# A gated graph layer on one core: completion counts of their own for two streams of transfers, and five groups of rows instead of two on the SyncE queue

## The chip, the cores and the metric

The kernel runs on one core of a Trainium2 chip. The core has five engines, each with an instruction queue of its own: PE (matrix products), DVE (vector work), ACT (activations and copies), POOL (which here only issues gathers) and SyncE, whose queue (SPq) issues nearly all plain transfers. Engines and transfers wait for one another by semaphores. The metric is device time in microseconds (us); lower is better.

## The reference

The layer works on a graph of 12,500 nodes with 128 features and 400,000 edges, which arrive sorted by their target node. Cut to what matters:

```python
h = jnp.maximum(_layernorm(x), 0.0)
s, d = src, dst                                            # 400,000 edges
m = relu(concat([h[s], h[d], edge_attr]) @ w1 + b1) @ w2 + b2
agg = segment_sum(m, d, num_segments=12500)
gi = agg @ w_ih + b_ih
gh = h @ w_hh + b_hh
r = sigmoid(gi_r + gh_r);  z = sigmoid(gi_z + gh_z)
n = tanh(gi_n + r * gh_n)
out = x + (1 - z) * n + z * h
```

## The kernel before

**Tiles.** A tile is 128 edges. 8 tiles make a group `k` (1024 edges); there are `NP` = 391 groups. The main loop runs over half-groups `u` from 0 to 781, here called half-steps, so group `k` belongs to half-steps 2k and 2k + 1. A first stage normalises the nodes, keeps them transposed on the chip (`hT_all`) and writes the products `h @ w1[0:128]` to a table `A` and `h @ w1[128:256] + b1` to a table `B`, both in device memory.

**What a group needs.** Since the edges are sorted by target, the targets of a group lie in a window of 32 nodes (two of them, 8 apart, for the two halves of the tiles).
- The window's rows of `B` are brought into a buffer `RW` by two transfers of 16 KB (`window_rows`, L602), four groups ahead; there are four such buffers.
- A buffer `L` (three of them, each for two groups) receives two transfers of 256 KB from `fetch`: the places of the targets (L563, from `dstP`: two rows, each repeated over 32 partitions) and the transposed edge features (L566, from `eaP`). `fetch(k // 2 + 3)` stands at half-step u = 2k of every second group, that is once in four half-steps, and waits until PE has used the buffer.
- DVE turns the places in `L` into a one-hot matrix (`onehot_T`, L575), three groups ahead of the group's last step. PE multiplies `L` by `RW` (L673), which gives the target's and the edge features' part of the message.
- The source's part, rows of `A`, comes in one of four ways, below. DVE adds it and applies the relu in one custom instruction (L701). PE then sums the messages per node by a one-hot product (L724), and every 14 groups a block of nodes is finished by a generator (`node`) that is advanced step by step.

**Four ways for the source's rows.** By default POOL gathers them: one indirect DMA for each tile (L156), 8 for a group, into one of 11 buffers `G`. A gather waits until the add of the group 11 earlier on POOL's list has freed its buffer. The table `SPREAD` takes some groups away from POOL and spreads them evenly over the loop: 27 to DVE and 28 to ACT, which copy the columns of `hT_all` one by one (L967, L960; PE multiplies them afterwards), and some to SyncE, which issues a transfer of 512 B for each of the 1024 rows (L952) into one buffer, `G_sp`. Before each 32 rows SyncE loads 32 row addresses into registers (L945).

**What sets the order.** The order is written out by hand: what each engine does follows the program. `run_jobs` spreads the work of a one-by-one group evenly over the half-steps between its start and its end, four phases to a half-step, four rows at a time for SyncE. A SyncE group `k` has to be through at half-step 2k - 8, and the next one starts at 2k + 2. The first starts at u = 24. `START` and `SPREAD` give the groups their places:

```python
lo, hi = START[m] // 2 + 2, NP - {"dve": 7, "act": 5, "sp": 12}[m]
for i in range(n):
    k = lo + int((i + 1) * (hi - lo) / n)
```

**Semaphores of transfers.** Unless told otherwise, every transfer that SyncE issues counts up one of eight semaphores, taken in turn. Before a transfer is issued, the one that used the same semaphore eight transfers earlier must have landed. All of SyncE's transfers are in one such ring: rows, windows, places, features, the nodes' loads and stores.

Of the kernel before, what the change touches and what calls it, by code (L numbers as in the profile page):

```python
# [11 lines left out]
I32 = mybir.dt.int32  # L12
# [5 lines left out]
ALU = mybir.AluOpType  # L18
# [11 lines left out]
V = 32  # L30
# [9 lines left out]
QP = 2  # L40
# [12 lines left out]
PIECE = 128  # L53
STEP = {"act": 4, "dve": 8, "sp": 4}
ROW = 4 * D
SPREAD = {"dve": 27, "act": 28, "sp": 2}
START = {"dve": 14, "act": 4, "sp": 24}
NR = 12672

# [4 lines left out]
def tile_gnn(ctx: ExitStack, tc: tile.TileContext, x, src, srcT, dstT, dstP, eaT, eaP, w1, b1, w2T, b2,  # L64
             wih, bih, whh, bhh, out):
    nc = tc.nc
# [23 lines left out]

    mode, order = {}, {m: [] for m in SPREAD}
    for m, n in SPREAD.items():
# [3 lines that stand above are left out]
# [171 lines left out]
    node_of = const.tile([2 * V, NP], F32, name="node_of")  # L267
# [75 lines left out]
    with tc.tile_pool(name="pp", bufs=3) as pp:  # L343
# [77 lines left out]
        def chunk(q):  # L421
            b, c = chunks[q]
            i0, n = bats[b]
            return b, i0, c, min(n, c + 4), PB(b), (i0 + c) * 128
# [4 lines left out]
        for q in range(NC + 3):  # L429
            if q < NC:  # L430
                b, i0, c, e, P, n0 = chunk(q)
# [3 lines left out]
            if 1 <= q <= NC:  # L435
                b, i0, c, e, P, n0 = chunk(q - 1)
# [6 lines left out]
            if q >= 3:  # L443
                b, i0, c, e, P, n0 = chunk(q - 3)
# [3 lines left out]
            if q < NC:  # L448
                b, i0, c, e, P, n0 = chunk(q)
# [4 lines left out]
            if 1 <= q <= NC:  # L454
                b, i0, c, e, P, n0 = chunk(q - 1)
# [12 lines left out]
            if q >= 3:  # L468
                b, i0, c, e, P, n0 = chunk(q - 3)
                if e == bats[b][1]:  # L470
                    nc.sync.dma_start(nodes(A, i0, e, P), asb[b][:P, :e, :])
            if 2 <= q <= NC + 1:
                b, i0, c, e, P, n0 = chunk(q - 2)
# [13 lines left out]
    dlast = p3.tile([128, BLOCKS[-1][1] + 128], F16, name="dlast", bufs=1)  # L487
# [63 lines left out]


    Ls, OH, RT, HE, SEG = ({} for _ in range(5))
    hand = {}

    def fetch(q):
        if q * QP >= NP:
            return
        n = min(QP, NP - q * QP)
        c = slice(q * QP * 512, (q * QP + n) * 512)  # L560
        Ls[q] = p3.tile([128, QP * 512], F32, name="L")
        p = dstP[:, c]
        nc.sync.dma_start(  # L563
            Ls[q].bitcast(I32)[:2 * V, :n * 512],
            bass.AP(tensor=p.tensor, offset=p.offset, ap=[list(p.ap[0]), [0, V], [1, n * 512]]))
        nc.sync.dma_start(Ls[q][2 * V:, :n * 512], eaP[:, c])  # L566

    def onehot_T(k):
        if k >= NP:
            return  # L570
        c = slice((k % QP) * 512, (k % QP + 1) * 512)
        o, i = Ls[k // QP][:2 * V, c], Ls[k // QP].bitcast(I32)[:2 * V, c]
        n = k - BLOCKS[-1][0]
        if n < 0:
            nc.vector.tensor_scalar(o, i, node_of[:, k:k + 1], None, op0=ALU.is_equal)  # L575
        else:
            nc.vector.tensor_scalar(o, i, node_of[:, k:k + 1], 0.0, op0=ALU.is_equal, op1=ALU.add,
                                    accum_out=dlast[:2 * V, n:n + 1])


    bases = {}
# [433 lines left out]
    for q in range(3):  # L1015
        fetch(q)
# [4 lines left out]
    def stages(u):  # L1021
        if u + 7 >= 0:
            raw_stats(u + 7)
        if u + 6 >= 0:
            raw_fin(u + 6)
            raw_h(u + 6)
        if u % 2 == 0:
            onehot_T(u // 2 + 3)
        elif u > -7:
            onehot(u // 2 + 3)  # L1030
        if u + 4 >= 0:
            raw_turn(u + 4)
        if u + 3 >= 0:
            pre(u + 3)
        if u + 2 >= 0:
            add(u + 2)
            relu(u + 2)
# [18 lines left out]
    for u in range(NU):  # L1056
        k, h = divmod(u, 2)
        gathers(u)
        if h == 0:
            window_rows(k + 4)  # L1060
            if k % QP == 0:
                fetch(k // QP + 3)
            if k and k == BLOCKS[block(k)][0]:
                nodes_left.append([node(block(k) - 1), 2 if k < BLOCKS[-1][0] else 1])
            if k % PLACE == 1:
                indices(k // PLACE + 2)
            if k % PLACE == 5:
                place(k // PLACE + 1)
                dst_tile(k // PLACE + 2)
            if k == 6:  # L1070
                late_setup()
            if k == 20:
                store_stats()
            if k == NP - 20:
                check_windows()
        if u == min(START.values()) - 2:
            nc.vector.tensor_scalar(at[:NJ, :], at[:NJ, :], place_of[:, 0:1], place_of[:, 1:2],
                                    op0=ALU.mult, op1=ALU.add)
# [123 lines left out]
    f = nc.values_load(flag[0:1, 0:1], min_val=0, max_val=1)  # L1202
# [67 lines left out]
```

## Time and profile before

| | |
|---|---|
| median of 3 runs | 3404.46 us (3404.36 to 3407.26) |
| the profiled execution | 3403.76 us |
| its span, first to last instruction | 3401.8 us |
| ACT busy | 3079.4 us |
| POOL busy | 2566.1 us |
| PE busy | 2417.4 us |
| DVE busy | 2225.1 us |
| gathers (POOL) | 2669 |
| single rows (SyncE) | 2048 |
| bytes moved | 335.44 MB |

The profile's first part lists busy time by engine. Instructions that only issue a transfer, load registers or wait are not counted as busy, so SyncE has no row there at all; its waits are an answer of their own, in which "SPq L952 <- DMA L<-in_dstP" reads: SyncE, at line 952, waited until the transfer into L from dstP had landed. Idle time of another engine ends either by a releaser, which is named, or by "issue", where the engine waited for nothing that the profile shows. A row of a group reads: line, engine, operation, output and inputs, count, then busy us, mean ns of one, idle us before them and what ended it.

### The profile page before, as it was taken

What the parts mean: (1) busy time and instruction counts of PE and PEld (TensorE: products, weight loads), DVE (VectorE), ACT (ScalarE), POOL (GpSimd) and SP (SyncE); (2) the same over time, 40 slices, a digit from 0 to 9 for tenths busy, and PEclk for the clock granted to TensorE, in tenths of its full rate; (3) what the DMA queues carried; (4) which work ended last, traced back from release to release, by engine and by line L of the source; (5) the groups of instructions that cost most, each with busy time, mean ns of one, the idle gap of its engine ahead of it and who ended that gap; (6) DMA issues with size and microseconds to landing.
All of it is one profiled execution on the core that took longest, in us unless ns stands there. A gap on an engine that the chain in (4) does not pass through costs nothing. (4 is left out here: it accounts for less than half of the span.)

```text
span 3401.8 us, 88642 instructions
## 1 busy us (share of the span) xinstructions
PE 2417.4 (71%) x13113; PEld 1563.7 (46%) x13113; DVE 2225.1 (65%) x16468; ACT 3079.4 (91%) x29057; POOL 2566.1 (75%) x2678
## 2 busy tenths in 40 slices
PE   7567777777677767776777667676677767766767
PEld 7444444444445444544444444444444434444445
DVE  8556666666676666666666666666666666666665
ACT  7699999999999998999899988988988898898984
POOL 7777777777777777777777777777777777777776
PEclk9777887887887778777877877788777778777878
DMA  6434444434443333343434433443433334343332
GB/s 213 106 88 93 97 100 99 101 94 100 102 98 94 98 99 95 95 101 97 98 93 99 98 94 93 96 96 93 98 93 92 95 94 99 92 97 96 92 92 73
DMA packets 191316, 335.44 MB, mean 99 GB/s; under 512 B 66753, under 2 KB 112384, under 8 KB 190729
## 3 DMA queue, kind: packets, MB, share of 16 engines
q0 software_dynamic: 85408, 175.09, 23.0%
q1 hardware_dynamic: 105177, 154.58, 16.4%
q14 instruction: 478, 3.92, 0.4%
q8 instruction: 109, 1.79, 0.2%
q10 hardware_dynamic: 144, 0.07, 0.0%
HBM read 309.24 MB, written 20.24 MB: 97 GB/s over the span
## 5 line engine op out<-in xcount | busy, mean ns | idle before, releaser
L156 POOL DMA_INDIRECT G<-A,src_i x2600 | 2498.9, 961 | 796.2 <-issue 753.7
L960 ACT COPY HE_act<-hT_all 128x4 uint8 x28672 | 2886.8, 189 | 51.4 <-issue 27.0
L967 DVE SCALAR_TENSOR_TENSOR both<-hT_all 128x4 uint16 x13824 | 1173.4, 153 | 988.5 <-issue 980.7
L673 PE MATMUL pre<-RW,L 128*128 128x256 f32 x3128 | 1132.4, 488 | 229.8 <-DVE RB L701 220.6
L673 PEld LDWEIGHTS pre<-RW,L 128*128 128x128 f32 x3128 | 660.6, 236 | 506.1 <-DVE RB L701 234.0
L724 PE MATMUL seg<-RB,OH 128*32 128x129 f32 x6250 | 603.9, 324 | 380.0 <-DVE RB L701 349.7
L724 PEld LDWEIGHTS seg<-RB,OH 128*32 128x32 f32 x6250 | 333.1, 125 | 820.4 <-DVE RB L701 532.7
L701 DVE CUSTOM_DVE_ANT_0 RB<-pre,G 128x1024 f32<-128x1024 f32 (+1 forms) x326 | 394.5, 1210 | 62.7 <-DMA G<-A,src_i 49.2
L575 DVE TENSOR_SCALAR L<-L,node_of 64x512 f32<-64x512 int32 x382 | 186.7, 489 | 9.7 <-DMA L<-in_dstP 9.4
L719 PE MATMUL seg<-zrow 1*128 1x129 bf16 x196 | 45.3, 231 | 164.4 <-DVE OH L623 164.2
L623 DVE TENSOR_TENSOR OH<-dloc,seg 128x256 f32<-128x256 f16 (+1 forms) x392 | 159.5, 407 | 0.5 <-issue 0.5
L750 PE MATMUL nd<-spot,sums 128*128 128x40 f32 x782 | 116.6, 321 | 1.2 <-DVE sums L733 1.2
L750 PEld LDWEIGHTS nd<-spot,sums 128*128 128x128 f32 x782 | 112.4, 231 | 10.5 <-issue 9.0
L710 ACT ACTIVATE RB<-pre 128x1024 f32<-128x1024 f32 x64 | 65.0, 1015 | 52.4 <-PE pre L684 52.4
L809 ACT ACTIVATE gt<-nd 128x512 f32<-128x512 f32 (+2 forms) x28 | 16.4, 585 | 96.5 <-PE nd L803 96.5
L972 DVE COPY HE_dve<-both 128x512 uint8<-128x512 uint8 x216 | 96.6, 447 | 7.4
L684 PEld LDWEIGHTS pre<-w1a,HE_act 128*128 128x128 f32 x448 | 88.4, 245 | 11.6
L684 PEld LDWEIGHTS pre<-w1a,HE_dve 128*128 128x128 f32 x432 | 87.9, 252 | 12.1
L684 PE MATMUL pre<-w1a,HE_act 128*128 128x128 f32 x448 | 86.4, 327 | 0.0
L684 PE MATMUL pre<-w1a,HE_dve 128*128 128x128 f32 x432 | 85.1, 333 | 0.0
L156 POOL DMA_INDIRECT G<-in_x,src_i x69 | 65.9, 954 | 21.8 <-issue 20.7
L233 PE MATMUL nd<-w1b,hT_all 128*128 128x128 f32 x224 | 45.5, 346 | 43.3 <-DVE xb L835 43.3
(177 smaller groups left out, 1383.9 us busy)
## 6 DMA issues: line engine op xcount, KB each, us to landing
L<-in_dstP SPq DMA_DIRECT2D x195, 256.0 KB
L<-in_eaP SPq DMA_DIRECT2D x195, 256.0 KB
G<-A,src_i POOLq DMA_INDIRECT x2600
G_sp<-A SPq DMA_DIRECT2D x2048, 0.5 KB
RW<-B SPq DMA_DIRECT2D x782, 16.0 KB
xb<-in_x SPq DMA_DIRECT2D x26, 256.0 KB
out<-xb SPq DMA_DIRECT2D x26, 256.0 KB
xs<-in_x SPq DMA_DIRECT2D x11, 512.0 KB
```

The costliest lines, as they stand in the source:

```text
L156: nc.gpsimd.indirect_dma_start(out=G[k][:, j, a, :], out_offset=None, in_=table, in_offset=bass.IndirectOffsetOnAxis(ap=src_i[c][:, i:i + ...
L575: nc.vector.tensor_scalar(o, i, node_of[:, k:k + 1], None, op0=ALU.is_equal)
L623: nc.vector.tensor_tensor(o, d.to_broadcast(shape), i.to_broadcast(shape), op=ALU.is_equal)
L673: nc.tensor.matmul(p[:, 2 * i:2 * i + 2, :], Ls[k // QP][:, c0:c0 + 128], RW[k % 4], start=True, stop=not raw)
L684: nc.tensor.matmul(p[:, 2 * i + a, :], cols, w1a, start=False, stop=n + 1 == len(l) or l[n + 1][1] != j)
L701: nc.vector._custom_dve(TENSOR_ADD_SAT, out=o, in0=p, in1=G[k].rearrange("p j a f -> p (j a) f")[:, c, :], s0=float("inf"), s1=0.0)
L710: nc.scalar.activation(o, p, AF.Relu)
L724: nc.tensor.matmul(p[r0:r0 + V, :D + 1], OH[k][:, j, a, :], RB[k % 2][:, 2 * j + a, :D + 1], start=False, stop=all(b != a for _, _, b in r ...
L750: nc.tensor.matmul(p[:, bass.ds(offs[i], V + SHIFT)], sums[:, slot(b, i), :D], spot[:, i % 2, :], start=False, stop=i == len(offs) - 1)
L960: nc.scalar.copy(he[:, e * 4:e * 4 + 4], column(v))
L967: nc.vector.scalar_tensor_tensor(both[:, (e0 % PIECE + i) // 2, :], column(vals[i + 1]), 256.0, column(vals[i]), op0=ALU.mult, op1=ALU.add)
L972: nc.vector.tensor_copy(he[:, p0 * 4:(p0 + PIECE) * 4].rearrange("p (n c b) -> p n c b", c=2, b=4), both.bitcast(U8).rearrange("p n (b c) ...
```

## The change

The change has two parts. The places and features of `L` no longer count up the ring of eight: each of the three buffers gets a semaphore of its own, which both transfers of a fetch raise by 16, and DVE waits for it explicitly before the first one-hot of the buffer. And SyncE gets five groups in place of two; by the code above these are 87, 160, 233, 306 and 379 where they were 196 and 379. The groups of DVE and ACT stay where they are.

```diff
-SPREAD = {"dve": 27, "act": 28, "sp": 2}
+SPREAD = {"dve": 27, "act": 28, "sp": 5}
...
+    landed = [tc.alloc_semaphore(f"landed{i}") for i in range(3)]
...
     def fetch(q):
...
-        nc.sync.dma_start(
-            Ls[q].bitcast(I32)[:2 * V, :n * 512],
-            bass.AP(tensor=p.tensor, offset=p.offset, ap=[list(p.ap[0]), [0, V], [1, n * 512]]))
-        nc.sync.dma_start(Ls[q][2 * V:, :n * 512], eaP[:, c])
+        for fetched in (
+                nc.sync.dma_start(
+                    Ls[q].bitcast(I32)[:2 * V, :n * 512],
+                    bass.AP(tensor=p.tensor, offset=p.offset, ap=[list(p.ap[0]), [0, V], [1, n * 512]])),
+                nc.sync.dma_start(Ls[q][2 * V:, :n * 512], eaP[:, c])):
+            fetched.then_inc(landed[q % 3], 16)
+            tc.no_tile_sem_insts.add(fetched.ins.name)
+            tc.add_to_no_dep_group(f"places{q}", fetched.ins)
 
     def onehot_T(k):
         if k >= NP:
             return
+        q = k // QP
+        if k % QP == 0:
+            nc.vector.wait_ge(landed[q % 3], 32 * (q // 3 + 1))
...
+        tc.declare_no_dep(made.ins, group=f"places{q}", reason="behind the wait for the landing")
+        if k % QP == 0:
+            tc.declare_fence(made.ins, group=f"places{q}")
```

More of the change, by code (lines that the diff above doesn't have):

```diff
@@ L574, in onehot_T @@
         if n < 0:
-            nc.vector.tensor_scalar(o, i, node_of[:, k:k + 1], None, op0=ALU.is_equal)
+            made = nc.vector.tensor_scalar(o, i, node_of[:, k:k + 1], None, op0=ALU.is_equal)
         else:
-            nc.vector.tensor_scalar(o, i, node_of[:, k:k + 1], 0.0, op0=ALU.is_equal, op1=ALU.add,
-                                    accum_out=dlast[:2 * V, n:n + 1])
+            made = nc.vector.tensor_scalar(o, i, node_of[:, k:k + 1], 0.0, op0=ALU.is_equal, op1=ALU.add,
+                                           accum_out=dlast[:2 * V, n:n + 1])
+        tc.declare_no_dep(made.ins, group=f"places{q}", reason="behind the wait for the landing")
+        if k % QP == 0:
+            tc.declare_fence(made.ins, group=f"places{q}")
     bases = {}
```

## The prediction

> **What bounds the kernel now.** I read the page first, then the stretches of the span engine by engine, then who waited for whom, and last SyncE's own waits, which the page does not list among its engines.
>
> ```profile
> span 3401.8 us, 88642 instructions
> PE 2417.4 (71%) x13113; PEld 1563.7 (46%) x13113; DVE 2225.1 (65%) x16468; ACT 3079.4 (91%) x29057; POOL 2566.1 (75%) x2678
> L156 POOL DMA_INDIRECT G<-A,src_i x2600 | 2498.9, 961 | 796.2 <-issue 753.7
> ```
>
> ACT has the largest share, but POOL is the engine that never rests: its idle time is put down to "issue", the gap that its own sequencer leaves between two gathers. One gather costs (2498.9 + 796.2) / 2600 = 1.267 us. The stretches (PE, PEld, DVE, ACT, POOL, each with its count) confirm it:
>
> ```profile
> 400.00:800.00 400.00, 295.01 (x1616) 188.22 (x1615) 275.20 (x2095) 386.22 (x3777) 303.04 (x315) 0.82 0.41 98
> 1200.00:1600.00 400.00, 288.11 (x1559) 186.00 (x1558) 267.95 (x2050) 374.74 (x3651) 303.66 (x317) 0.80 0.39 97
> 2800.00:3200.00 400.00, 278.71 (x1493) 174.94 (x1493) 257.78 (x1948) 359.74 (x3465) 303.41 (x318) 0.77 0.39 95
> ```
>
> POOL issues 315 to 318 gathers in every 400 us, while ACT falls from 386 to 360: ACT has room, POOL has none. The sum of waits agrees from the other side, since the add on DVE does run into gathered rows that have not landed:
>
> ```profile
> DVE RB L701 <- DMA G<-A,src_i: 49.2, 31, 3.7
> ```
>
> So POOL's row of gathers sets the time, and every other engine follows at a distance. Next comes SyncE's queue (SPq). These are its waits while it brings rows one by one, and the rows (tile G_sp) with their first and last start:
>
> ```profile
> SPq L952 <- DMA L<-in_dstP: 865.4, 150, 8.1
> SPq L563 <- PE pre L673: 180.4, 55, 14.1
> SPq L952 <- DMA L<-in_eaP: 89.1, 170, 1.5
> SPq L602 <- DMA L<-in_dstP: 71.5, 13, 6.9
> SPq L602 <- DMA B<-xb: 56.3, 24, 3.1
> SPq L563 <- PE pre L684: 54.7, 9, 13.2
> SPq L119 <- DMA L<-in_dstP: 46.4, 8, 6.7
> SPq L108 <- DMA L<-in_dstP: 36.4, 6, 6.8
> SPq L602 <- PE pre L673: 20.9, 13, 4.2
> ```
>
> ```profile
> L952 SPq MOVE G_sp<-A x2048: 29/29/38, 229.9 to 3276.3; - x187
> L952 SPq DMA_DIRECT2D G_sp<-A x2048: 224/228/643, 229.9 to 3276.4; - x187
> ```
>
> The stretch is 3276.3 - 229.9 = 3046.4 us long. In it SyncE waits 865.4 + 71.5 + 46.4 + 36.4 = 1019.7 us for the places (L from dstP) to land, 89.1 us for the features (L from eaP), and 180.4 + 54.7 + 20.9 = 256.0 us for PE. Only the last is slack: there SyncE is early. The other 3046.4 - 1019.7 - 89.1 - 256.0 = 1681.6 us are its instructions and small waits (B's store of 56.3 us among them). SyncE, no engine of the page's first part, is thus taken for 2790 of 3046 us and is the second limit, close behind POOL.
>
> **The change, part by part.** *Gathers.* Three groups of 8 tiles leave POOL: 24 gathers x 1.267 = 30.4 us less. As long as nothing else is slower, that is the gain. The add on DVE reads G_sp in place of G and costs the same.
>
> *Rows.* By the code, SyncE's groups are now 196 and 379, and become 87, 160, 233, 306 and 379. The first still starts at half-step u = 24 and the last still has to be through by u = 2 x 379 - 8 = 750, so 5120 rows stand where 2048 stood, in the same 726 half-steps of the program. The price of a row and of its registers:
>
> ```profile
> 1536.45 1.21 SPq L952 DMA_DIRECT2D G_sp<-A  x4
> ```
>
> ```profile
> L945 SPq TENSOR_LOAD <-at x64: 1876/2142/2377, 227.6 to 3229.5; - x64
> L945 DVEq EVENT_SEMAPHORE  x1: 21/21/21, 188.1 to 188.1; - x1
> ```
>
> Four rows back to back take 1.21 us from the first start to the last end, and the last lasts 0.228, so one row every (1.21 - 0.228) / 3 = 0.327 us. 3072 more rows are 1005 us, and 96 more loads of 32 registers at 2.142 us are 206 us. SyncE's work becomes 1681.6 + 1005 + 206 = 2893 us, against 3046.4 - 30.4 = 3016 us that POOL's new pace would leave it. It fits, with 123 us over, only if the waits for places and features go. Everything hangs on that.
>
> *Semaphores.* Places and features leave the ring of eight semaphores. A transfer of the ring waits until the one eight before it has landed; so far, six transfers could follow a pair of L before the seventh waited for the places. Here is that, in one fetch:
>
> ```profile
> 1505.43 0.58 SPq L563 DMA_DIRECT2D L<-in_dstP  x1
> 1506.07 0.51 SPq L566 DMA_DIRECT2D L<-in_eaP  x1
> 1506.68 10.14 SPq L952 DMA_DIRECT2D G_sp<-A  x8
> 1517.93 0.35 SPq L740 DMA_DIRECT2D xb<-in_x  x1
> ```
>
> Eight rows take 10.14 us where 8 x 0.327 = 2.6 would do. After the change eight transfers can follow, and the ninth waits for the first of these eight. So the question is when that first row lands, and the packets answer it (first line: 1509.6 to 1513.6 us; second: its hardware queue; third: 1514.5 to 1514.7 us):
>
> ```profile
> DMA packets 150, 0.38 MB, mean 95 GB/s; under 512 B 60, under 2 KB 60, under 8 KB 149
> ```
>
> ```profile
> q1 hardware_dynamic: 34, 0.14, 10.7%
> ```
>
> ```profile
> DMA packets 15, 0.01 MB, mean 56 GB/s; under 512 B 7, under 2 KB 13, under 8 KB 15
> ```
>
> Six rows are issued by 1506.68 + 6 x 0.36 = 1509. In the four microseconds from 1509.6 no packet of 512 B moves at all (the counts under 512 B and under 2 KB are both 60); the queue moves 34 packets in 0.14 MB, the 4 KB pieces of L. Then, within 0.2 us, 13 - 7 = 6 packets of 512 B move: the six rows, together, behind L. They land when the places land. The wait therefore does not go; it changes its name, from the places to the first row behind them.
>
> [...]
>
> What it becomes: there are 726 / 4 = 182 fetches in the stretch, so 1019.7 / 182 = 5.6 us each today. Two more transfers pass before the stop, 2 x 0.327 = 0.65 us: 4.95 us if the first row lands with the places, and 0.52 us more (89.1 / 170, how much later the features land) if it lands behind the features. I take the middle, 5.2 us, or 946 us. The features' own 89.1 us go.
>
> *The explicit wait on DVE.* 196 instructions of about 0.021 us, 4 us on an engine that is not the limit: nothing. The same wait stood on L575 before; behind it in DVE's queue stand the one-hot, the adds and DVE's share of hand-made columns, which PE and ACT await. If DVE were the limit it would cost those 4 us; less than nothing it cannot cost, since the instruction it frees still waits for the same landing. Three more index rows in the preamble go out before the stretch, beside the transposes and loads of the first stage; exposed, they would cost 3 x 0.327 = 1 us.
>
> *Sum.* 2893 + 946 = 3839 us for the stretch: SyncE becomes the bound, its 256 us of slack are used up, and PE and DVE wait for windows (RW) and places that it issues late. Two corrections. L shares its DMA engines with POOL's gathers, and POOL slows to about 3046 / 3839 = 0.8 of its rate. In the quiet window the 34 packets occupied 0.107 x 16 x 4.0 = 6.85 us, or 0.20 us each; if L's tail stands on two engines, one for each of the two rows of places, they took 4.0 x 2 / 34 = 0.235 us for each; over 36 packets that is 1.2 us per fetch if POOL were gone altogether, and some more since a packet itself is stretched. With a fifth of POOL gone I take 0.45 us per fetch, 82 us in all (ends: 0 and 310, the latter for 1.7 us each). And SyncE starts the stretch ahead of its users: L is asked for 6 half-steps before its one-hot, 6 x 3046 / 726 = 25 us, and takes some 10 to land, so 15 us pass before anyone waits. So 3839 - 82 - 15 = 3742 us, 696 us more than now: a span of 3401.8 + 696 = 4098 us. The profiled execution took 3403.76 us with its span of 3401.8, and the median of the runs is 3404.46, so the same within 1 us; I say 4095.
>
> **Rivals.** *The wait really goes* (faster). If rows behind L landed in their usual time, SyncE would need 2893 us plus little, POOL would stay the bound, and the time would be 3404 - 30 = 3374 us. For it speaks that 1109 us of waiting carry L's name. Against it stand the packets above. It decides where the stall per fetch falls under (3016 - 2893) / 182 = 0.7 us, from 5.6 today; at 0.85 us the gain is just gone.
>
> *L lands far sooner.* With POOL waiting for buffers in turns, L could have its DMA engines to itself: at 1.7 to 3 us less per fetch the stretch is 310 to 550 us shorter, and the time 3630 to 3870 us. For it: gathers and L do run beside each other. Against it: the POOL work per group stays, and it is only spread over a fifth more time.
> [...]
>
> *More than the sum.* If the first row always lands behind the features and POOL's slowing brings nothing, the stretch is 2893 + 182 x 5.5 = 3894 us, and the time 4240.
>
> **How the numbers follow.** Main case, SyncE the bound and 3870 to 4260 us: 0.84. L much sooner, 3630 to 3870: 0.06. The wait goes, 3374: 0.08. Both cancel at about 3404: 0.02. Runs of this kernel agree to about 0.1%, so 0.2% is about what can be told from no change. Faster 0.08, same 0.02, slower 0.90. The range of 8 in 10 is the main case with its bounds: 3840 to 4270.
>
> **What would show it.** Right: SyncE's waits name G_sp or RW where they named L, some 5 us per fetch; its waits for PE all but vanish; POOL waits for RB's add; the last row starts near 3970 instead of 3276.3; PE and DVE wait for RW or L. [...]

## The result, and the profile after

The changed kernel takes 4172.09 us (median of 4 runs, 4165.45 to 4174.29), the one before 3405.17 us on the same chip: a ratio of 1.225, 95% interval 1.2235 to 1.2264. It is slower by 767 us. The main case of the prediction, SyncE's queue as the bound, came about; its 4095 us were 77 us too low.

The page of the changed kernel, by engine, and the groups whose idle time tells most (busy, mean ns of one, idle before and its releaser):

```profile
span 4172.5 us, 94686 instructions
PE 2550.5 (61%) x13113; PEld 1623.6 (39%) x13113; DVE 2235.3 (54%) x16468; ACT 3086.7 (74%) x29057; POOL 2535.9 (61%) x2654
L156 POOL DMA_INDIRECT G<-A,src_i x2576 | 2468.6, 958 | 1506.7 <-DVE RB L712 747.0
L684 PE MATMUL pre<-RW,L 128*128 128x256 f32 x3128 | 1244.3, 529 | 1443.2 <-DMA RW<-B 1277.7
L583 DVE TENSOR_SCALAR L<-L,node_of 64x512 f32<-64x512 int32 x382 | 188.3, 493 | 726.6 <-DMA L<-in_eaP 726.1
```

The busy time of ACT, DVE and POOL is what it was, to within 1.2%; only the span grew. POOL, which waited 2.6 us for the add before, now waits 747.0 us for it to free a buffer. PE waits 1277.7 us for windows and DVE 726.1 us for L: all of them wait for what SyncE issues late. PE's granted clock is lower too (0.746 in the mean, 0.796 before) and its busy time 5.5% longer; but PE is busy for 61% of the span, and SyncE hardly waits for it any more, as its waits further down show. POOL's pace in two stretches (the POOL column is the fifth after the length) falls from 317 gathers in 400 us to about 250:

```profile
1200.00:1600.00 400.00, 230.67 (x1178) 141.01 (x1178) 203.32 (x1542) 277.04 (x2692) 238.61 (x250) 0.74 0.31 75
2800.00:3200.00 400.00, 227.16 (x1156) 142.54 (x1155) 203.68 (x1548) 296.84 (x2856) 234.84 (x245) 0.72 0.31 75
```

SyncE's own waits while it brings rows, from 230 to 4071 us, and the rows' first and last start:

```profile
SPq L963 <- DMA G_sp<-A: 881.0, 170, 8.1
SPq L613 <- DMA B<-xb: 57.9, 26, 3.6
SPq L565 <- PE pre L684: 22.3, 13, 8.0
SPq L565 <- PE pre L695: 13.0, 2, 12.5
SPq L247 <- DMA RW<-B: 7.7, 1, 7.7
SPq L963 <- DMA RW<-B: 7.3, 3, 4.2
SPq L613 <- PE pre L684: 6.0, 5, 4.8
```

```profile
L963 SPq MOVE G_sp<-A x5120: 29/29/39, 230.2 to 4071.0; - x197
```

None of SyncE's waits carries L's name any more. Instead SyncE waits 881.0 us, 170 times, for rows of its own. The stretch is 4071.0 - 230.2 = 3840.8 us where it was 3046.4, and the waits for PE, which were 256.0 us, have shrunk to 22.3 + 13.0 + 6.0 = 41.3 us.

### The profile page after: what moved, and what is told of

Its sections match the earlier page's. It is cut to its first block, busy times and chain, and to the rows that moved or that the text cites. A ratio compares the mean times of both kernels' runs of the same rounds, so it can differ in the third digit from the quotient of the medians.

```text
span 4172.5 us, 94686 instructions
## 1 busy us (share of the span) xinstructions
PE 2550.5 (61%) x13113; PEld 1623.6 (39%) x13113; DVE 2235.3 (54%) x16468; ACT 3086.7 (74%) x29057; POOL 2535.9 (61%) x2654
## 2 busy tenths in 40 slices
DMA packets 196745, 335.84 MB, mean 80 GB/s; under 512 B 69444, under 2 KB 118147, under 8 KB 196111
## 3 DMA queue, kind: packets, MB, share of 16 engines
q0 software_dynamic: 84640, 173.51, 18.4%
## 5 line engine op out<-in xcount | busy, mean ns | idle before, releaser
L156 POOL DMA_INDIRECT G<-A,src_i x2576 | 2468.6, 958 | 1506.7 <-DVE RB L712 747.0
L684 PE MATMUL pre<-RW,L 128*128 128x256 f32 x3128 | 1244.3, 529 | 1443.2 <-DMA RW<-B 1277.7
L684 PEld LDWEIGHTS pre<-RW,L 128*128 128x128 f32 x3128 | 726.1, 259 | 1755.6 <-issue 1350.1
L735 PE MATMUL seg<-RB,OH 128*32 128x129 f32 x6250 | 619.7, 331 | 75.3 <-DVE RB L712 55.6
L583 DVE TENSOR_SCALAR L<-L,node_of 64x512 f32<-64x512 int32 x382 | 188.3, 493 | 726.6 <-DMA L<-in_eaP 726.1
L712 DVE CUSTOM_DVE_ANT_0 RB<-pre,G 128x1024 f32<-128x1024 f32 x323 | 392.6, 1216 | 28.9 <-PE pre L684 24.9
L810 PE MATMUL nd<-DEG,brow 34*128 34x512 f32 (+2 forms) x112 | 77.7, 780 | 4.9 <-ACT gt L820 4.5
L814 PE MATMUL nd<-TOT,w2ih 128*128 128x512 f32 (+2 forms) x112 | 72.1, 732 | 0.0
## 6 DMA issues: line engine op xcount, KB each, us to landing
L<-in_dstP SPq DMA_DIRECT2D x195, 256.0 KB
L<-in_eaP SPq DMA_DIRECT2D x195, 256.0 KB
xb<-in_x SPq DMA_DIRECT2D x26, 256.0 KB
out<-xb SPq DMA_DIRECT2D x26, 256.0 KB
```

The source lines that it names most:

```text
L156: nc.gpsimd.indirect_dma_start(out=G[k][:, j, a, :], out_offset=None, in_=table, in_offset=bass.IndirectOffsetOnAxis(ap=src_i[c][:, i:i + ...
L583: made = nc.vector.tensor_scalar(o, i, node_of[:, k:k + 1], None, op0=ALU.is_equal)
L684: nc.tensor.matmul(p[:, 2 * i:2 * i + 2, :], Ls[k // QP][:, c0:c0 + 128], RW[k % 4], start=True, stop=not raw)
L712: nc.vector._custom_dve(TENSOR_ADD_SAT, out=o, in0=p, in1=G[k].rearrange("p j a f -> p (j a) f")[:, c, :], s0=float("inf"), s1=0.0)
L735: nc.tensor.matmul(p[r0:r0 + V, :D + 1], OH[k][:, j, a, :], RB[k % 2][:, 2 * j + a, :D + 1], start=False, stop=all(b != a for _, _, b in r ...
L810: nc.tensor.matmul(pg, brow[:, c], DEG[:, :w], start=True, stop=False)
```

## Experiments

**The semaphores alone.** Two groups as before:

```diff
-SPREAD = {"dve": 27, "act": 28, "sp": 5}
+SPREAD = {"dve": 27, "act": 28, "sp": 2}
```

In the expectations from here on, a ring that rows share with L is not the ring of eight semaphores. It stands for the hardware queue q1 of the profile: in the fetch of the prediction q1's 34 packets from 1509.6 to 1513.6 us are L's, and the rows' six of 512 B are among its 13 from 1514.5 to 1514.7 us.

> Two groups of rows as before, semaphores of L as after. Theory (a row issued behind L shares a ring with it and lands when L lands): the time stays at 3405 us within 0.3%, since POOL is the bound in both, and SyncE's waits only change their name: about 1110 us in the name of L become 850 to 1000 us in the name of G_sp and RW. Rival (the semaphores free SyncE): the time is the same too, but SyncE waits less than 250 us for any transfer, and its waits for PE rise from 256 us to over 1000.

Measured: 3402.76 us against 3400.49, ratio 1.0003 (0.9993 to 1.0013): no difference. SyncE's waits in its stretch:

```profile
SPq L963 <- DMA G_sp<-A: 525.1, 99, 8.5
SPq L613 <- DMA G_sp<-A: 379.9, 63, 8.9
SPq L565 <- PE pre L684: 282.3, 70, 14.2
SPq L613 <- DMA B<-xb: 60.5, 28, 3.6
SPq L751 <- DMA G_sp<-A: 54.9, 12, 6.6
SPq L613 <- PE pre L684: 52.0, 22, 5.8
SPq L565 <- PE pre L695: 49.2, 7, 13.5
```

525.1 + 379.9 + 54.9 = 959.9 us of waiting for rows stand where 1109 us of waiting for L stood; the waits for PE rise from 256 to 383.5 us. The semaphores by themselves free about 130 to 150 us of SyncE's queue, not a thousand. The wait changes its name, and the rival in which it goes has fallen.

**The five groups alone.** The kernel before with the same one line changed from 2 to 5, L on the ring of eight.

> Five groups of rows, semaphores as before. Theory: SyncE is the bound, and the stall at each L is whole, 5.6 us for the places and 0.5 for the features, where the changed kernel has about 5.2: 2893 + 1020 + 89 = 4002 us of stretch against the changed kernel's 3841, so about 4330 us. Rival (the semaphores do nothing at all): 4172 us. Rival (it is the new semaphores and the explicit wait on DVE that cost the time, not the rows): near 3405 us.

Measured: 4360.59 us against 3400.49, ratio 1.281 (1.2767 to 1.2853).

```profile
SPq L952 <- DMA L<-in_dstP: 984.1, 172, 8.8
SPq L952 <- DMA L<-in_eaP: 92.1, 170, 1.5
SPq L602 <- DMA B<-xb: 56.8, 26, 3.1
```

```profile
L952 SPq MOVE G_sp<-A x5120: 29/29/39, 231.3 to 4260.5; - x197
```

The stretch is 4029.2 us (4002 expected), the time 31 us above the 4330 expected, and both rivals are far off. The slowdown comes from the rows; the semaphores win back 4029.2 - 3840.8 = 188 us of it.

**The places in two transfers.** If the rows stand behind L on one queue, L's time on it must be made shorter. In the same fetch, from 1506.6 to 1508.9 us, the queue moved

```profile
q1 hardware_dynamic: 70, 0.27, 39.8%
```

or 0.398 x 16 = 6.4 packets at a time; the 34 from 1509.6 to 1513.6 us, at 10.7%, are 1.7 at a time. By the trace's packets, over all fetches of the kernel before, 12.4 of the queue's 4 KB packets run at once 3 us after the places' transfer starts, and 2.0 after 6 us. The places are two rows, each repeated, into 64 partitions. That the two rows make this thin end, and that a transfer for each row would run more of its pieces at once, was my estimate; no run had shown it. The same bytes, then, in one more transfer, with DVE's wait raised to match:

```diff
-                nc.sync.dma_start(
-                    Ls[q].bitcast(I32)[:2 * V, :n * 512],
-                    bass.AP(tensor=p.tensor, offset=p.offset, ap=[list(p.ap[0]), [0, V], [1, n * 512]])),
+                *(nc.sync.dma_start(
+                    Ls[q].bitcast(I32)[V * a:V * (a + 1), :n * 512],
+                    dstP[a:a + 1, c].to_broadcast([V, n * 512])) for a in range(2)),
...
-            nc.vector.wait_ge(landed[q % 3], 32 * (q // 3 + 1))
+            nc.vector.wait_ge(landed[q % 3], 48 * (q // 3 + 1))
```

> The changed kernel, with the places as two transfers of 32 partitions, one for each row, in place of one of 64 partitions. [...] The stall goes, the stretch is 2893 us + 182 x 0.6 for the third transfer = 3002 us, which just fits POOL's 3016, and the time is 3370 to 3420 us. Rival (rows wait for something other than their ring, the general load of the DMA engines): the same bytes move, so about 4172 us plus 182 x 0.6 = 4280.

Measured: 3373.97 us against 3400.49, ratio 0.9917 (0.9897 to 0.9937). It beats both kernels, the one before by 0.8%. SyncE's waits in its stretch, its rows, and POOL's pace in one stretch:

```profile
SPq L613 <- DMA B<-xb: 57.2, 26, 3.3
SPq L565 <- PE pre L684: 47.9, 15, 11.4
SPq L963 <- DMA G_sp<-A: 44.5, 83, 1.2
SPq L565 <- PE pre L695: 13.8, 3, 7.9
SPq L613 <- PE pre L684: 11.8, 6, 5.5
```

```profile
L963 SPq MOVE G_sp<-A x5120: 29/29/38, 214.8 to 3252.3; - x197
```

```profile
1200.00:1600.00 400.00, 283.87 (x1528) 181.22 (x1528) 266.20 (x2022) 372.26 (x3603) 303.51 (x317) 0.80 0.38 98
```

Waiting for rows falls from 881.0 to 44.5 us with the same five groups, and POOL is back at 317 gathers in 400 us. By the trace's landings, the first row behind L lands 4.8 us after the places' transfer starts (median over the fetches that a row follows), where it took 10.2 us in the changed kernel. What held the rows was the shape of the places' transfer, not the general load: the bytes are the same (335.84 MB in the changed kernel, 335.88 here). The semaphores differ too: until a transfer of the places has landed, its semaphore rises in 3 steps at most in the kernel before, and in up to 16 where the same kernel has the split. For a single row it rises in 2 at most. How many DMA engines a transfer had, the profile does not record.

**The split alone.** The same split in the kernel before, with two groups and the shared semaphores.

> The kernel before with the same split of the places, its two groups and the shared semaphores kept. Theory: the time stays at 3405 us within 0.3% (POOL is the bound), and SyncE's waits in the name of L fall from 1109 us to under 250, its waits for PE rise by about as much. Rival (SyncE's stalls already cost the kernel before something): 20 us or more are gained.

Measured: 3399.68 us against 3400.49, ratio 0.9996 (0.9987 to 1.0006). Over the whole span:

```profile
SPq L563 <- PE pre L672: 900.4, 158, 13.2
SPq L601 <- PE pre L672: 362.1, 67, 18.0
SPq L951 <- DMA L<-in_eaP: 98.9, 116, 2.5
```

About a thousand microseconds of SyncE's queue change from stalls behind L into waits for PE, and the time does not move: SyncE was not the bound of the kernel before. POOL was: the add on DVE still waits for gathered rows, for 42.2 us here and 49.2 us in the kernel before, and the split kernel, with 24 gathers fewer, is 26.5 us faster.

```profile
DVE RB L700 <- DMA G<-A,src_i: 42.2, 29, 4.3
```

**Fewer gathers beside L.** One correction of the prediction was that L lands sooner when POOL slows. Here POOL gathers half of the tiles from group 40 on; the messages of the other half lack their source's part.

```diff
+        if k >= 40:
+            nc.gpsimd.memset(G[k][:, :, 1, :], 0.0)
         for u in (2 * k, 2 * k + 1):
             for t, j, a in unit_tiles(u):
+                if k >= 40 and a:
+                    continue
```

> The changed kernel, but from group 40 on POOL gathers only every other tile of its groups (those of the first half of the window) and clears the rest with one memset, so the messages of the cleared tiles lack their source's part; it is there to see how much POOL's gathers hold up L. Half of the gather traffic is gone beside L. Theory of the prediction (L shares its DMA engines with the gathers and lands sooner when they thin out, up to 1.7 us per fetch if all were gone): 0.6 to 0.9 us less stall per fetch, 881 us of waiting for rows becomes 730 to 780, and the time 4020 to 4070 us. [...]

Measured in one execution: 4090.01 us. SyncE's waits for rows, and what the two queues moved:

```profile
SPq L967 <- DMA G_sp<-A: 818.5, 170, 7.9
```

```profile
q1 hardware_dynamic: 111327, 156.18, 14.1%
q0 software_dynamic: 46880, 96.10, 10.5%
```

The gathers fall from 173.51 to 96.10 MB, and the wait from 881.0 to 818.5 us, 0.37 us a stop; the time falls by 82 us. Beside L itself, too, they are halved: 4 to 12 us after L is issued, 13.9 packets of the gathers' queue start per microsecond, where 26.0 did in the changed kernel. The expectation missed: the effect is there, at about half the size I gave it. The first row behind L lands after 9.8 us (mean) in place of 10.2, so L's pace is mostly its own.

**Three and four groups.** The changed kernel with "sp": 3, and with 4.

> The changed kernel with three groups of rows in place of five. Theory: each group costs SyncE 1024 x 0.327 + 32 x 2.142 = 403 us, so its work is 2893 - 2 x 403 = 2086 us, plus 182 x 5.2 = 946 us of stalls: 3032 us, just what POOL's pace (3046 - 10 = 3036) leaves. The time is at the knee, 3390 to 3440 us. Rival (the cost is not in proportion to the rows but comes with the new placing of the groups from 87 on): near the five groups' 4172 us, or near 3395 us with SyncE waiting for PE more than before.

> The changed kernel with four groups of rows. Theory: 403 us of SyncE's work per group on top of a full queue, so one group less than five takes 403 us off the stretch of 3841: 3438 us, and the time is 4172 - 403 = 3769 us, within 30 us. Rival (the stalls grow with the rows behind L): more than 30 us off this line.

Measured: 3463.16 us with three (ratio 1.0155, 1.0115 to 1.0195) and 3814.61 us with four, in one execution. SyncE's rows, three groups first, then four:

```profile
L963 SPq MOVE G_sp<-A x3072: 29/29/39, 232.5 to 3348.9; - x192
```

```profile
L963 SPq MOVE G_sp<-A x4096: 29/29/39, 230.4 to 3702.7; - x196
```

The stretches are 3116.4, 3472.3 and 3840.8 us for three, four and five groups, so a group costs 356 and 368 us, not the 403 of its instructions, and both points lie above the line (by 23 us over the range's end, and by 46 us). Both expectations missed, and the rivals for three groups lie further off still. The price of the rows held: without the waits for rows and for PE the stretches differ by 388 and 404 us. The stalls did not stay as they were, but against the rival they grow with fewer rows. With three groups waiting behind L is

```profile
SPq L613 <- DMA G_sp<-A: 719.1, 124, 8.8
SPq L963 <- DMA G_sp<-A: 122.4, 25, 7.7
SPq L751 <- DMA G_sp<-A: 101.6, 23, 6.2
```

943.1 us, against 922.0 with four and 881.0 with five. The stall is a landing that has to be waited out, and what SyncE does meanwhile comes off it: by the traces' landings, a stop is 3.6 us long with five groups where SyncE loads registers between L and the stop, and 5.5 us where it does not. But that does not explain the difference, for with three groups such loads fall before 48 of 179 stops and with five before 49 of 181. Most of it lies in the stops without a load, 5.9 us with three groups and 5.5 with five. Why these shorten stays open.

**The split with the shared semaphores.** Five groups and two transfers for the places, but L back on the ring of eight semaphores; against the split kernel it tells what semaphores of its own are worth once the first row lands after 4.8 us in place of 10.2.

> Five groups, the places split in two transfers, but L on the eight shared semaphores as before. Theory: with the ring free again L lands after about 4 us, and the seventh transfer behind it waits about 0.7 us for the features, as in the kernel before with the split places (98.9 us in 116 waits); 170 such waits are 120 to 150 us, more than the 73 us that SyncE has left over in the split kernel with its own semaphores. So the queue is just full: 3385 to 3450 us, against 3374 with the own semaphores. Rival (once the ring is free the own semaphores bring nothing): 3374 us.

Measured: 3437.15 us against 3402.22, ratio 1.0106 (1.0089 to 1.0122), inside the expected range.

```profile
SPq L951 <- DMA L<-in_eaP: 131.5, 117, 2.5
```

131.5 us of waiting for features are more than SyncE had left, and the kernel is slower than the one before, where with its own semaphores it is faster (ratio 0.9917). The first part of the change does pay, but only where SyncE's queue is full: by about 63 us here, by 188 us with the places in one transfer (the five groups alone), and by nothing with two groups.

Here POOL's pace misleads. It still issues 317 or 318 gathers in 400 us, as in the split kernel, and ends no later; these are the gathers of the split kernel, then of this one, with their first and last start:

```profile
L156 POOL DMA_INDIRECT G<-A,src_i x2576: 940/947/1528, 92.7 to 3354.4; - x199
L156 POOL DMA_INDIRECT G<-A,src_i x2576: 940/944/1548, 92.8 to 3345.6; - x199
```

But after the last gather the split kernel (span 3375.0 us) takes 21 us more, and this one (span 3435.0 us) 89. With 11 buffers POOL runs ahead while the rest falls behind. What tells is the add's wait for gathered rows, 49.2 us in the kernel before and 0.2 us here:

```profile
DVE RB L700 <- DMA G<-A,src_i: 0.2, 1, 0.2
```

## Why the prediction was right, and where it was off

*What bounds the kernel.* Right. POOL was the bound (the split alone and the semaphores alone change SyncE's waits by hundreds of microseconds and not the time), and SyncE was the second limit, close behind. Of the two signs that I gave, the add's waits for gathered rows are the good one; POOL's even pace is none by itself, since the split with the shared semaphores has the same pace and POOL is not its bound.

*The gain of 30 us.* Right, though the change itself never sees it: the split kernel, where POOL is the bound again, is 3400.49 - 3373.97 = 26.5 us faster, where 24 gathers were put at 30.4 us.

*Rows.* I put SyncE's work, with small waits, at 2893 us. After the change it is 3840.8 - 881.0 - 41.3 = 2918 us: 25 us, or 0.9%, above. Prices taken from a few rows held over 3072 more of them.

*The semaphores.* Right, and the step on which all hung: the wait moved from L to the first row behind it. Forecast 946 us before the correction and 864 after; measured 881.0 us. The stops are 170 and not 182, since not each fetch ends in one, at 5.2 us each as taken. That the sum came within 17 us of 864 is luck: 12 stops fewer, 62 us, stood in for the 82 us of a correction of which little came.

*The correction for POOL's slowing.* Wrong in size. I took 82 us off because L would land 0.45 us sooner. The first row lands after 10.2 us in the changed kernel, after 10.3 in the one before and 10.5 with the semaphores alone (means over the fetches), so 0.1 to 0.3 us came of it at most. Halving the gathers brings 0.37 us a stop; for a fifth less that is, in proportion, about 0.15 us (an estimate), so 0.45 was three times too much. The two engines and the 36 packets from which I worked it out no run shows, since the profile does not name a packet's engine; what it shows of L's end is the 1.7 packets at a time from 1509.6 to 1513.6 us. Besides, the slowed gathers do not thin out evenly: by the trace's packets, 4 to 12 us after L is issued some 26 packets of the gathers' queue start per microsecond against 29 before, and 15 to 18 us after it about 14 against 23. POOL rests where L is not.

*SyncE's slack.* I took all 256 us of waits for PE as used up; 41.3 us stayed. The head start of 15 us became 24: after the last row 4172.5 - 4071.0 = 101.5 us follow, where 3401.8 - 3276.3 = 125.5 did. In sum the forecast span of 4098 us missed 25 us of work, 881.0 - 864 = 17 of stalls and 41 of waits for PE, and had 9 too few of the head start: 25 + 17 + 41 - 9 = 74 us, the difference to 4172.5.

*DVE's explicit wait.* No cost seen, as forecast: the kernel with the semaphores alone is at a ratio of 1.0003.

*The rivals.* "The wait really goes" fell with the semaphores alone. "L lands far sooner" fell with the result, where the row behind L lands after 10.2 us in place of 10.3, and the half gathers show why: even they bring only 0.4 us. "More than the sum" put 4240 us for two things at once, of which one nearly held: POOL's slowing brought little. The other did not: in the kernel before, the first row lands 0.3 us behind the places and 0.6 us ahead of the features (means).

## What to carry to other kernels

A wait in the name of a transfer is not always for its semaphore: ask where the next transfer would land if it did not wait, and look for its packets. Giving L semaphores of its own changed who waits here (with them alone, 1109 us behind L became 959.9 us behind rows), not how soon the first row lands (after 10.3 us before, 10.5 with them alone). The shape of a transfer can decide how long the next one stands behind it: with the same bytes, 10.2 us with the places in one transfer and 4.8 us in two. And an engine that the page does not list can be the next bound, as SyncE was, taken for 2790 of 3046 us: add up its waits and its work over the stretch before giving it more. Nor does an engine's even pace show that it is the bound, as long as it has buffers to run ahead into (POOL issued 317 or 318 gathers in 400 us in the split kernel and in the slower one with the shared semaphores): look whether anyone waits for it.

## What was not expected of the hardware

The shape of one transfer of 256 KB decided between 4172 and 3374 us: as one transfer with a source of two repeated rows, it held the rows behind it for 10.2 us, and as two transfers of 32 partitions for 4.8 us, for 0.82 us of SyncE's time instead of 0.59. Halving the gathers that run beside it shortened its landing by only some 4% (the first row after 9.8 us, mean, in place of 10.2).
